# Weight chunks streamed as three tiles, the last weight split in place and later, and two kinds of fetch issued behind the chunks, in a two-layer graph network kernel

## Chip, core and metric

The kernel runs on one core of one Trainium2 chip. The metric is device time in microseconds for one execution of the whole program, here given as the median of three runs. The profile is that of one further execution, with the hardware profiler on.

## What is computed

The input is `x` with 32 graphs of 512 nodes and 512 features, and one adjacency `adj` of 512 x 512 that holds zeros and ones. Layer 0 is masked attention with 8 heads of 64 lanes, layer 1 a graph convolution; both add their input and normalise. Cut to what matters:

```python
q, k, v = (x @ W + b for W, b in ((Wq, bq), (Wk, bk), (Wv, bv)))       # 8 heads of 64
scores = q @ k.T / sqrt(64) + where(adj == 0, -1e9, 0)
x = layernorm(x + softmax(scores) @ v)
y = adj @ x
x = layernorm(x + y @ weight + bias)
```

## The kernel before

**Three passes.** A float32 product is made of three passes of TensorE matmuls at a reduced format. Each operand is split into three parts, named HIGH, REST and BOTH, and the passes multiply like parts: HIGH and REST add into a bank called near, BOTH into a bank called far. A split takes a scaled copy on ScalarE (HIGH), a combination on VectorE or GpSimd (REST), and one more, for the activations on GpSimd (BOTH). `one_pass` (line 417) issues four matmuls of 128 x 128 by 128 x 512, `three_passes` twelve.

**Chunks.** Wq and Wk are split once, at the start, into eight chunks in the order q0, k0, q1, k1, q2, k2, q3, k3 (`SEQUENCE`). A chunk is 768 KB: its three parts, of 256 KB each, in one tile of 6 KB per partition. `keep_chunk` (L404) stores each to DRAM as one transfer, and in every later graph `fetch_chunk` (L412) brings it back, as one transfer, into a ring of three tiles named `stream` (`AHEAD = 3`). The fetch of the chunk three places on is written directly after the matmuls that used the ring's oldest tile, so it waits for all twelve of them. The last three chunks of a graph are followed by the fetches of q0, k0, q1 for the next graph, which stand near the end of an iteration.

**Order of work.** The order on every engine is written out by hand (`manual_schedule`), and each engine runs its list in order. `iteration(b)` mixes the end of graph b's attention, the projections and first scores of graph b+1, and the convolution of graph b-1. TensorE's order in it is: attention with values for head pairs 0 and 1 (`attend`, L625); scores of the second group of head pairs (`scores`, L602); projections q0 to k1 of graph b+1 (L417); attention for head pairs 2 and 3; scores of graph b+1's first group; projections q2 to k3; values (L417 from `wv`); aggregation with the adjacency (L526); convolution with the last weight (L417 from `w`).

**Scores.** A score stage has 16 products into a ring of eight banks. VectorE empties each bank with the mask into an `e` tile (L604), ScalarE takes the exponential of each pair of them (L606), GpSimd adds the exponentials over the key blocks (L617). VectorE folds those sums in squares of 32 x 32 (`fold_squares`, L655 and L657); they go to DRAM and back to come to the right partitions (`pass_parts` L664, `fetch_parts` L671), and `add_up` (L677, L678) makes the inverse.

**Rows.** The attention's output comes out transposed. `turn_out` transposes it in squares on VectorE (L637) and stores it to DRAM (L639), `fetch_rows` (L645) reads it back as four transfers of 64 KB for each head pair, ScalarE scales it (L691) and GpSimd adds it to x (L695).

**SyncE's queue.** Nearly all transfers are issued by SyncE, in the order of the code, and one that waits holds up all behind it. In iteration b the order is: the two `turned` stores, `fetch_parts`, eight rows transfers, in iterations 2 to 5 an adjacency row (`load_adjacency_rows`, L290, looked at by L296 to L298 for a low half), the chunks k1, q2, k2, a store of the output, q3, then `load(b)`, k3, the squares of x for graph b+2 (16 transfers, L232), eight more rows transfers, and q0, k0, q1 for the next graph.

**The start.** Graph 0's projections use the chunks as they are made. Then come graph 0's first scores, its values, and the splits of x for graph 1 (L304 HIGH on ScalarE, L307 REST on VectorE, L310 BOTH on GpSimd), the first `fold_squares`, and the split of the last weight `W1` into `w1`: `load_last_weight` (L750) loads it as four tiles of 256 KB into room of the q and k tiles, `split_last_weight` does for each of four row blocks three ScalarE activations (L757, L758, L760, the last into a spare tile) and two GpSimd subtractions (L761, L762). All this stands ahead of iteration 0. `AFTER[b]` holds units that the next iteration runs between the transposes of its first two head pairs.

Of the kernel before, what the change touches and what calls it, by code (L numbers as in the profile page):

```python
# [8 lines left out]
FP = mybir.dt.float32  # L9
# [9 lines left out]
P = 128  # L19
# [163 lines left out]
def fast_kernel(ctx: ExitStack, tc, verdict, x, adj, Wq, bq, Wk, bk, Wv, bv, W1, b1, out):  # L183
# [20 lines left out]
    def plain(t):  # L204

        return t.bitcast(FP)
# [164 lines left out]
    MADE = {}  # L371

    def chunk():
        return work.tile([P, 3, DB, P], FR, name="stream", bufs=AHEAD)

    def make_chunk(n):

        which, m = SEQUENCE[n]
        if n < DB:
            made = early[:, n, :, :, :]  # L380
        elif n < DB + AHEAD:
            made = chunk()
        else:
            made = last_chunk
        MADE[n] = CHUNK[0, which, m] = made
        high_of_weight(made[:, HIGH, :, :], RAW[which, m // 2][:, m % 2, :, :])

    def rest_of_chunk(n):
        which, m = SEQUENCE[n]
        made = MADE[n]  # L390
        rest_of_weight(made[:, REST, :, :], made[:, HIGH, :, :], RAW[which, m // 2][:, m % 2, :, :])

    def both_of_chunk(n):
        made = MADE[n]
        both_of_weight(made[:, BOTH, :, :], made[:, HIGH, :, :], made[:, REST, :, :])

    def finish_chunk(n):
        rest_of_chunk(n)
# [1 line left out]

    def keep_chunk(n):
        which, m = SEQUENCE[n]
        KEPT[which, m] = passing.tile([P, 3, DB, P], FP, name=f"kept_{which}{m}", bufs=1)
        nc.sync.dma_start(KEPT[which, m], plain(MADE.pop(n)))  # L404

    def fetch_chunk(n):

        b, (which, m) = n // len(SEQUENCE), SEQUENCE[n % len(SEQUENCE)]
        if b >= B:
            return  # L410
        CHUNK[b, which, m] = chunk()
        nc.sync.dma_start(plain(CHUNK[b, which, m]), KEPT[which, m])  # L412

    def one_pass(f, pm, left, right, blocks=range(DB)):

        for d in blocks:
            nc.tensor.matmul(pm, left(f, d), right(f, d), start=(f != REST and d == 0),  # L417
                             stop=(f != HIGH and d == DB - 1))
# [12 lines left out]
    def project(b, which, m):  # L431

        n = b * len(SEQUENCE) + SEQUENCE.index((which, m))
        near, far = bank(N), bank(N)
        w, xt = CHUNK.pop((b, which, m)), XT[b]
        three_passes(near, far, lambda f, d: w[:, f, d, :], lambda f, d: xt[f][:, d, :])
        if b == 0:
            return [(finish_projection, b, which, m, near, far)]
        if (which, m) in SEQUENCE[:-AHEAD]:
            fetch_chunk(n + AHEAD)  # L440
        finish_projection(b, which, m, near, far)

    def project_first_two():

        ends = []
        xt = XT[0]
        for which, m in SEQUENCE[:2]:
            ends.append((CHUNK[0, which, m], bank(N), bank(N)))
        for f in (HIGH, REST, BOTH):
            for w, near, far in ends:  # L450
                one_pass(f, far if f == BOTH else near, lambda f, d: w[:, f, d, :], lambda f, d: xt[f][:, d, :])
# [189 lines left out]
    def fetch_rows(b, hp):  # L641
        rows = ROWS[b, hp] = work.tile([P, NB, P], FP, name="rows")
        turned = TURNED.pop((b, hp)).rearrange("(i r) (c j f) -> j r c i f", r=SQ, c=NB, f=SQ)
        for j in range(P // SQ):
            nc.sync.dma_start(rows[j * SQ:(j + 1) * SQ, :, :].rearrange("p c (i f) -> p c i f", f=SQ), turned[j])  # L645
# [99 lines left out]
    both_of_chunk(1)  # L745

    def load_last_weight():
        for d in range(DB):
            RAW["w1", d] = work.tile([P, D], FP, name="raw", tag="qk"[d % 2] + "0", bufs=PAIRS)
            nc.sync.dma_start(RAW["w1", d], W1[d * P:(d + 1) * P, :])  # L750

    def values_weight(d):
        return RAW["v", d // 2][:, d % 2, :]

    def split_last_weight(d):
        w = RAW.pop(("w1", d))
        nc.scalar.activation(w, w, AF.Copy, scale=1.0 / EPSILON)  # L757
        nc.scalar.activation(w1[:, HIGH, d, :], w, AF.Copy, scale=SHRINK)  # L758
        temp = work.tile([P, N], FR, name="temp", tag="turn", bufs=TURNS)
        nc.scalar.activation(temp, w, AF.Copy, scale=EPSILON * SHRINK)  # L760
        nc.gpsimd.tensor_sub(w1[:, REST, d, :], w, plain(w1[:, HIGH, d, :]))  # L761
        nc.gpsimd.tensor_sub(w1[:, BOTH, d, :], plain(w1[:, REST, d, :]), plain(temp))  # L762

    def norm(t, which):

# [30 lines left out]
    def iteration(b):  # L796
# [16 lines left out]
            fetch_parts(b, 0)  # L813
        take_scores(b, 1)
        run(later)
        fetch_rows(b, 0)
        fetch_rows(b, 1)
        look = []
        if 2 <= b < 2 + NB:
            load_adjacency_rows(b - 2)  # L820
            look = [(look_for_low_half, b - 2)]
        if b == 0:
            run(merge(units[:4], [[(fold_squares, b, 1), (pass_parts, b, 0), (fetch_parts, b, 0)], [], [(add_up, b, 0)],
                                  folded[:1]]))
        else:
            old, young = norm(b - 1, 1), norm(b - 1, 0)
            roots = slice(0, 2 * NB if b > 1 else NB)
            if b == 1:
                run(survey(0, 0))
            run(merge(units[:4], [[(square_root, b - 1, roots), (add_up, b, 0), (invert_root, b - 1, roots)],  # L830
                                  folded[:1] + old[2:], [(store, b - 2)] if b > 1 else [], young[2:] + scaled]))
        attend(b, 2)
        turn_out(b, 2)
        load(b)
        attend(b, 3)
        turn_out(b, 3)
        if b == 0:
# [9 lines left out]
                          turned[:1] + (later_added if b == B - 2 else [])]))  # L847
        if b == B - 2:
            load(B - 1)
        run(merge(gathered, [[unit] for unit in turned[1:]]))  # L850
        fresh, seen, shift = survey(b, 0), survey(b - 1), biases(b - 1)
        high, rest, both = divided
# [166 lines left out]
```

## Time and profile before

| What | Value |
|---|---|
| Median of three runs | 2574.64 us (2574.56 to 2575.02) |
| The profiled execution | 2578.16 us |
| Span of the profiled execution, first to last instruction | 2575.9 us |
| Mean granted TensorE clock | 0.999 |
| SyncE's transfers, share of 16 DMA engines | 51.3%, 377.48 MB |
| Chunk fetches (L412) | 248 of 768 KB, 3.9 / 4.7 / 10.1 us to landing (least, median, most) |
| Rows transfers (L645) | 496 of 64 KB, median 2.4 us to landing |
| Loads of the last weight (L750) | 4 of 256 KB, median 8.6 us to landing |

A line of the page's fifth part or of a timeline reads: line of the code, engine, operation, what is written and what is read by the program's names, shapes, and how often. A timeline line begins with the start and the length in us, neighbours of one kind merged; in brackets is the engine's idle time before it and what ended it. PE is TensorE, DVE is VectorE, ACT is ScalarE, POOL is GpSimd, SPq is SyncE's queue, whose length is that of the issue alone. One score product counts as two matmuls in the trace.

### The profile page before, as it was taken

What the parts mean: (1) busy time and instruction counts of PE and PEld (TensorE: products, weight loads), DVE (VectorE), ACT (ScalarE), POOL (GpSimd) and SP (SyncE); (2) the same over time, 40 slices, a digit from 0 to 9 for tenths busy, and PEclk for the clock granted to TensorE, in tenths of its full rate; (3) what the DMA queues carried; (4) which work ended last, traced back from release to release, by engine and by line L of the source; (5) the groups of instructions that cost most, each with busy time, mean ns of one, the idle gap of its engine ahead of it and who ended that gap; (6) DMA issues with size and microseconds to landing.
All of it is one profiled execution on the core that took longest, in us unless ns stands there. A gap on an engine that the chain in (4) does not pass through costs nothing.

```text
span 2575.9 us, 35702 instructions
## 1 busy us (share of the span) xinstructions
PE 2562.7 (99%) x11324; PEld 1693.9 (66%) x11324; DVE 2058.9 (80%) x3795; ACT 1527.3 (59%) x2540; POOL 1751.0 (68%) x1105
## 2 busy tenths in 40 slices
PE   9999999999999999999999999999999999999998
PEld 6566666766667666666667666676766667666666
DVE  8778788787787887878878778887788787887878
ACT  5666655657556665556665566655656556565555
POOL 5766676666766666766667667676766766666767
PEclk9999999999999999999999999999999999999999
DMA  9655554655545545456454464454654545545431
GB/s 267 165 158 142 159 146 125 174 140 162 148 112 167 152 151 162 110 154 176 135 160 119 143 178 136 153 138 129 172 141 161 143 117 167 145 157 164 103 124 52
DMA packets 675042, 380.47 MB, mean 148 GB/s; under 512 B 586912, under 2 KB 591264, under 8 KB 674848
## 3 DMA queue, kind: packets, MB, share of 16 engines
q1 hardware_dynamic: 674416, 377.48, 51.3%
q8 instruction: 92, 1.51, 0.2%
q14 instruction: 102, 0.84, 0.1%
q10 hardware_dynamic: 432, 0.66, 0.1%
HBM read 303.57 MB, written 74.45 MB: 147 GB/s over the span
## 4 chain that ended last, share of the span: by engine, by line
PE 94%; DVE 2%; DMA 1%; POOL 1%; ACT 1%; issue 0%; SPq 0%; DVEq 0%; ACTq 0%; POOLq 0%
PE bank L417 52%; PE bank L602 17%; PE bank L625 16%; PE bank L526 9%; DVE e L604 1%; DMA stream<-kept_k 0%; DMA turned<-attT 0%; DVE bnst L477 0%; DVE factors L307 0%; POOL es L617 0%; ACT e L606 0%; SPq L645 0%; POOL factors L310 0%; PE bank L729 0%; POOL wv L932 0%
## 5 line engine op out<-in xcount | busy, mean ns | idle before, releaser
L417 PE MATMUL bank<-factors,stream 128*128 128x512 f32 x3012 | 704.3, 392 | 2.9 <-DMA stream<-kept_k 2.3
L606 ACT ACTIVATE e<-e 128x1024 f32<-128x1024 f32 x512 | 525.3, 1055 | 300.7 <-DVE e L604 262.3
L417 PEld LDWEIGHTS bank<-factors,stream 128*128 128x128 f32 x3012 | 560.1, 188 | 167.7 <-DVE e L604 23.5
L617 POOL TENSOR_TENSOR es<-es,e 128x1024 f32<-128x1024 f32 x256 | 615.9, 2406 | 20.1
L604 DVE SCALAR_TENSOR_TENSOR e<-gap,bank 128x512 f32<-128x512 uint8 x1024 | 617.6, 678 | 12.1 <-PE bank L602 12.1
L617 POOL TENSOR_TENSOR es<-e 128x1024 f32<-128x1024 f32 x128 | 305.8, 2389 | 425.6 <-ACT e L606 425.6
L602 PE MATMUL bank<-q,k 64*128 64x512 f32 x2048 | 464.9, 598 | 0.7 <-DVE attT L637 0.7
L625 PE MATMUL bank<-e,v 128*64 128x512 f32 x2048 | 453.6, 595 | 0.0
L602 PEld LDWEIGHTS bank<-q,k 64*128 64x128 f32 x2048 | 204.1, 186 | 259.9 <-issue 157.3
L417 PE MATMUL bank<-w,factors 128*128 128x512 f32 x1536 | 354.4, 389 | 0.5 <-POOL factors L310 0.5
L417 PE MATMUL bank<-wv,factors 128*128 128x512 f32 x1536 | 353.5, 389 | 0.0
L310 POOL TENSOR_TENSOR factors<-factors,factors 128x512 fp32r<-128x512 f32 x255 | 322.1, 1284 | 33.9 <-DVE factors L307 32.0
L691 ACT ACTIVATE rows<-rows,zero,inverse 128x64 f32<-128x64 f32 x992 | 335.0, 429 | 9.7 <-DVE inverse L678 9.7
L417 PEld LDWEIGHTS bank<-w,factors 128*128 128x128 f32 x1536 | 288.0, 188 | 61.3 <-POOL factors L310 1.3
L417 PEld LDWEIGHTS bank<-wv,factors 128*128 128x128 f32 x1536 | 288.2, 188 | 60.6 <-DVE e L604 0.8
L625 PEld LDWEIGHTS bank<-e,v 128*64 128x64 f32 x2048 | 141.4, 137 | 278.4 <-issue 265.4
L503 ACT ACTIVATE high<-xs 128x512 fp32r<-128x512 f32 x124 | 74.4, 627 | 333.3 <-PE bank L526 333.2
L504 POOL TENSOR_TENSOR low<-xs,high 128x512 fp32r<-128x512 f32 x124 | 159.2, 1295 | 156.3 <-PE bank L526 156.3
L541 POOL TENSOR_TENSOR xs<-xs,b_r 128x512 f32<-128x512 f32 x124 | 159.8, 1289 | 125.3 <-DVE xs L561 125.3
L637 DVE STREAM_TRANSPOSE attT<-bank 128x512 f32<-128x512 f32 x124 | 87.6, 708 | 159.1 <-PE bank L625 159.1
L493 ACT ACTIVATE xs<-xs,shift,rstd 128x512 f32<-128x512 f32 x248 | 181.5, 805 | 14.7 <-DVE shift L488 14.7
L695 POOL TENSOR_TENSOR xs<-xs,rows 128x512 f32<-128x512 f32 x124 | 160.6, 1306 | 22.6 <-ACT rows L691 14.9
(98 smaller groups left out, 2433.4 us busy)
## 6 DMA issues: line engine op xcount, KB each, us to landing
stream<-kept_q SPq DMA_DIRECT2D x124, 768.0 KB, 5.9
stream<-kept_k SPq DMA_DIRECT2D x124, 768.0 KB, 4.3
xin<-in_x_dram SPq DMA_DIRECT2D x496, 64.0 KB, 2.3
turned<-attT SPq DMA_DIRECT2D x124, 256.0 KB, 3.2
rows<-turned SPq DMA_DIRECT2D x496, 64.0 KB, 2.4
xs<-in_x_dram SPq DMA_DIRECT2D x31, 1024.0 KB, 6.1
out_dram<-xs SPq DMA_DIRECT2D x31, 1024.0 KB, 5.1
part<-passed SPq DMA_DIRECT2D x256, 8.0 KB, 1.7
```

Of the source, the lines that this page charges most:

```text
L310: engine.tensor_sub(both, plain(high), plain(rest))
L417: nc.tensor.matmul(pm, left(f, d), right(f, d), start=(f != REST and d == 0), stop=(f != HIGH and d == DB - 1))
L493: nc.scalar.activation(row, row, AF.Identity, bias=SHIFT[t][:, slot:slot + 1], scale=RSTD[t][:, slot:slot + 1])
L526: nc.tensor.matmul(pm, part, adjT[:, n % NB, :], start=(n == 0), stop=(n == 2 * NB - 1))
L541: nc.gpsimd.tensor_add(X[b][:, c, :], X[b][:, c, :], b1_r)
L602: nc.tensor.matmul(ps[s], keys[:, j * P:(j + 1) * P], queries, start=True, stop=True)
L604: nc.vector.scalar_tensor_tensor(e[:, s, :], gap[:, j, :], NEG * root, ps[s], op0=ALU.mult, op1=ALU.add)
L606: nc.scalar.activation(e, e, AF.Exp, scale=1.0 / root)
L617: nc.gpsimd.tensor_add(ES[b, hp], ES[b, hp] if j > 1 else E[b, hp, 0], E[b, hp, j])
L625: nc.tensor.matmul(po[s * HD:(s + 1) * HD, :], V[b, j][:, h * HD:(h + 1) * HD], e[:, s, :], start=(j == 0), stop=(j == NB - 1))
L691: nc.scalar.activation(part, part, AF.Identity, bias=zero, scale=inverse[:, c, s:s + 1])
L695: nc.gpsimd.tensor_add(cols, cols, ROWS.pop((b, hp)))
```

## The change

Four edits. A chunk becomes three tiles, each with a ring of three (`stream0`, `stream1`, `stream2`) and a transfer of its own, to DRAM and back. The last weight is loaded as one tile of 1 MB into the ring of the x tiles (`xs`), its split runs in iteration 0 behind graph 1's values, and BOTH is made from HIGH, scaled back into the raw tile in place, where a third copy of the raw weight was used. Ahead of iteration 0 only HIGH of graph 1's x is split; REST and BOTH run in iteration 0 between the first two transposes. And in iteration 1 both rows fetches, in iterations 2 to 5 the second of them, are issued behind the first projection with its chunk fetch, and the adjacency row behind `load(b)`.

```diff
     def chunk():
-        return work.tile([P, 3, DB, P], FR, name="stream", bufs=AHEAD)
+        return [work.tile([P, DB, P], FR, name=f"stream{f}", bufs=AHEAD) for f in (HIGH, REST, BOTH)]
...
     def keep_chunk(n):
         which, m = SEQUENCE[n]
-        KEPT[which, m] = passing.tile([P, 3, DB, P], FP, name=f"kept_{which}{m}", bufs=1)
-        nc.sync.dma_start(KEPT[which, m], plain(MADE.pop(n)))
+        KEPT[which, m] = [passing.tile([P, DB, P], FP, name=f"kept_{which}{m}_{f}", bufs=1) for f in range(3)]
+        for kept, made in zip(KEPT[which, m], MADE.pop(n)):
+            nc.sync.dma_start(kept, plain(made))
...
         CHUNK[b, which, m] = chunk()
-        nc.sync.dma_start(plain(CHUNK[b, which, m]), KEPT[which, m])
+        for part, kept in zip(CHUNK[b, which, m], KEPT[which, m]):
+            nc.sync.dma_start(plain(part), kept)
...
-        three_passes(near, far, lambda f, d: w[:, f, d, :], lambda f, d: xt[f][:, d, :])
+        three_passes(near, far, lambda f, d: w[f][:, d, :], lambda f, d: xt[f][:, d, :])
...
     def load_last_weight():
-        for d in range(DB):
-            RAW["w1", d] = work.tile([P, D], FP, name="raw", tag="qk"[d % 2] + "0", bufs=PAIRS)
-            nc.sync.dma_start(RAW["w1", d], W1[d * P:(d + 1) * P, :])
+        RAW["w1"] = work.tile([P, DB, D], FP, name="xs", bufs=2)
+        nc.sync.dma_start(RAW["w1"], W1.rearrange("(c p) f -> p c f", p=P))
...
-    def split_last_weight(d):
-        w = RAW.pop(("w1", d))
-        nc.scalar.activation(w, w, AF.Copy, scale=1.0 / EPSILON)
-        nc.scalar.activation(w1[:, HIGH, d, :], w, AF.Copy, scale=SHRINK)
-        temp = work.tile([P, N], FR, name="temp", tag="turn", bufs=TURNS)
-        nc.scalar.activation(temp, w, AF.Copy, scale=EPSILON * SHRINK)
-        nc.gpsimd.tensor_sub(w1[:, REST, d, :], w, plain(w1[:, HIGH, d, :]))
-        nc.gpsimd.tensor_sub(w1[:, BOTH, d, :], plain(w1[:, REST, d, :]), plain(temp))
+    def split_last_weight():
+        w = RAW["w1"]
+        for d in range(DB):
+            nc.scalar.activation(w[:, d, :], w[:, d, :], AF.Copy, scale=1.0 / EPSILON)
+            nc.scalar.activation(w1[:, HIGH, d, :], w[:, d, :], AF.Copy, scale=SHRINK)
+            nc.gpsimd.tensor_sub(w1[:, REST, d, :], w[:, d, :], plain(w1[:, HIGH, d, :]))
+        for d in range(DB):
+            nc.scalar.activation(w[:, d, :], plain(w1[:, HIGH, d, :]), AF.Copy, scale=EPSILON)
+            nc.gpsimd.tensor_sub(w1[:, BOTH, d, :], plain(w1[:, REST, d, :]), w[:, d, :])
...
         take_scores(b, 1)
         run(later)
-        fetch_rows(b, 0)
-        fetch_rows(b, 1)
-        look = []
-        if 2 <= b < 2 + NB:
-            load_adjacency_rows(b - 2)
-            look = [(look_for_low_half, b - 2)]
+        waiting = [(fetch_rows, b, 0), (fetch_rows, b, 1)]
+        looking = 2 <= b < 2 + NB
+        look = [(look_for_low_half, b - 2)] if looking else []
+        ready = 1 if looking else 0 if b == 1 else 2
+        run(waiting[:ready])
...
-            run(merge(units[:4], [[(square_root, b - 1, roots), (add_up, b, 0), (invert_root, b - 1, roots)],
+            run(merge(units[:4], [waiting[ready:]
+                                  + [(square_root, b - 1, roots), (add_up, b, 0), (invert_root, b - 1, roots)],
...
         load(b)
+        if looking:
+            load_adjacency_rows(b - 2)
         attend(b, 3)
...
         if b == B - 2:
             load(B - 1)
+        if b == 0:
+            split_last_weight()
         run(merge(gathered, [[unit] for unit in turned[1:]]))
...
     high, rest, both = splits_of_x(1)
-    run(high + rest + both[::-1])
-
+    run(high)
     fold_squares(0, 0)
-    run([(split_last_weight, d) for d in range(DB)])
+    AFTER[-1] = (rest + both[::-1], [])
     for b in range(B - 1):
         iteration(b)
```

More of the change, by code (lines that the diff above doesn't have):

```diff
@@ L379, in make_chunk @@
         if n < DB:
-            made = early[:, n, :, :, :]
+            made = [early[:, n, f, :, :] for f in (HIGH, REST, BOTH)]
         elif n < DB + AHEAD:
@@ L383, in make_chunk @@
         else:
-            made = last_chunk
+            made = [last_chunk[:, f, :, :] for f in (HIGH, REST, BOTH)]
         MADE[n] = CHUNK[0, which, m] = made
-        high_of_weight(made[:, HIGH, :, :], RAW[which, m // 2][:, m % 2, :, :])
+        high_of_weight(made[HIGH], RAW[which, m // 2][:, m % 2, :, :])
     def rest_of_chunk(n):
@@ L390, in rest_of_chunk @@
         made = MADE[n]
-        rest_of_weight(made[:, REST, :, :], made[:, HIGH, :, :], RAW[which, m // 2][:, m % 2, :, :])
+        rest_of_weight(made[REST], made[HIGH], RAW[which, m // 2][:, m % 2, :, :])
     def both_of_chunk(n):
         made = MADE[n]
-        both_of_weight(made[:, BOTH, :, :], made[:, HIGH, :, :], made[:, REST, :, :])
+        both_of_weight(made[BOTH], made[HIGH], made[REST])
     def finish_chunk(n):
@@ L450, in project_first_two @@
             for w, near, far in ends:
-                one_pass(f, far if f == BOTH else near, lambda f, d: w[:, f, d, :], lambda f, d: xt[f][:, d, :])
+                one_pass(f, far if f == BOTH else near, lambda f, d: w[f][:, d, :], lambda f, d: xt[f][:, d, :])
         return [(finish_projection, 0, which, m, near, far) for (which, m), (w, near, far) in zip(SEQUENCE, ends)]
```

## The prediction, made before the changed kernel was run

> **What bounds the kernel now.** I read the page first: busy shares and the chain of work that ended last.
>
> ```profile
> span 2575.9 us, 35702 instructions
> PE 2562.7 (99%) x11324; PEld 1693.9 (66%) x11324; DVE 2058.9 (80%) x3795; ACT 1527.3 (59%) x2540; POOL 1751.0 (68%) x1105
> ...
> PE 94%; DVE 2%; DMA 1%; POOL 1%; ACT 1%; issue 0%; SPq 0%; DVEq 0%; ACTq 0%; POOLq 0%
> ```
>
> TensorE is the bound. A change that leaves its matmuls alone can only win the time in which it stands still or is held back, and busy time hides some of that, so I read the TensorE timeline next, taking a stage's length as the distance between two starts.
>
> ```profile
> 56.91 8.27 PE L602 MATMUL bank<-q,k 64*128 64x512 f32 x32
> 65.11 11.17 PE L417 MATMUL bank<-factors,stream 128*128 128x512 f32 x48
> ...
> 83.23 2.85 PE L602 MATMUL bank<-q,k 64*128 64x512 f32 x12
> 86.74 6.48 PE L602 MATMUL bank<-q,k 64*128 64x512 f32 x20 [0.66 <-DVE attT L637]
> 93.15 11.22 PE L417 MATMUL bank<-factors,stream 128*128 128x512 f32 x48
> ...
> 122.19 7.21 PE L602 MATMUL bank<-q,k 64*128 64x512 f32 x32
> 129.33 8.49 PE L417 MATMUL bank<-factors,stream 128*128 128x512 f32 x36
> 139.52 2.97 PE L417 MATMUL bank<-factors,stream 128*128 128x512 f32 x12 [1.70 <-DMA stream<-kept_k]
> 142.42 7.09 PE L625 MATMUL bank<-e,v 128*64 128x512 f32 x32
> ```
>
> From iteration 6 on every stage repeats (scores 7.14, first four projections 11.15, period 79.6), so nothing is to be had there. The excess lies in the first iterations: scores from 56.91 take 8.20 (**A**, 1.06 over), scores from 83.23 take 9.92 (**B**, 2.78 over), projections from 129.33 take 13.09 (**C**, iteration 1, 1.94 over). Read the same way, the stages at 210.89, 290.77 and 450.84 (iterations 2, 3, 5) take 11.42, 12.03 and 11.93: 0.27, 0.88 and 0.78 over (**D**, 1.93). Sum 7.71 us, or 0.30%.
>
> Who is late in A and B is in the VectorE and then the ScalarE timeline:
>
> ```profile
> 51.24 4.41 DVE L307 SCALAR_TENSOR_TENSOR factors<-factors,turn 128x512 fp32r<-128x512 f32 x4
> ...
> 59.18 9.61 DVE L604 SCALAR_TENSOR_TENSOR e<-gap,bank 128x512 f32<-128x512 uint8 x16
> ...
> 82.60 0.27 DVE L677 TENSOR_REDUCE inverse<-part 128x16 f32<-128x64 f32 x1 [3.38 <-DMA part<-passed]
> ...
> 87.20 9.62 DVE L604 SCALAR_TENSOR_TENSOR e<-gap,bank 128x512 f32<-128x512 uint8 x16
> ```
>
> ScalarE:
>
> ```profile
> 59.85 0.63 ACT L757 ACTIVATE raw<-raw 128x512 f32<-128x512 f32 x1 [7.88 <-DMA raw<-in_L_gnn_weight_dram]
> ...
> 66.68 7.68 ACT L606 ACTIVATE e<-e 128x1024 f32<-128x1024 f32 x8
> ```
>
> A score stage has 16 products and eight banks, and L604 empties one per 0.60. In undisturbed stages the first L604 starts 1.16 after the stage (122.19 to 123.35, 203.75 to 204.91). In A it is 2.27, in B 3.97: 1.11 and 2.81 more, the same as the excess within 0.05. So **a score stage loses what its first L604 is late beyond 1.16**. In B the root is the split of the last weight: ScalarE waited 7.88 for it and worked at it until 66.68, exponentials and q, k came after it, VectorE's q at 74.96, the sums' round trip through DRAM (part<-passed) at 82.60.
>
> C is in SyncE's timeline:
>
> ```profile
> 121.40 1.97 SPq L639 DMA_DIRECT2D turned<-attT  x2
> ...
> 129.07 5.32 SPq L645 DMA_DIRECT2D rows<-turned  x8
> 134.48 0.57 SPq L412 DMA_DIRECT2D stream<-kept_k  x1
> ```
>
> The eight rows transfers stand ahead of the fourth chunk (k1). It is issued 5.15 after the stage starts, lands after 4.90 at 139.38, and TensorE resumes 0.14 later. In iterations 2, 3 and 5 the chunk is issued on time (at 213.94, 293.86, 453.93) but takes 5.3 to 5.9 behind rows and the adjacency row; it too lands 0.14 before its use. Iteration 4 takes 4.59 and iteration 7 3.97, and there nothing waits.
>
> **What the Trainium skill says.** "TensorE: Matmul & The Clock Gate", "Back-to-back issue gap", gives N/2.4 + 2.5 ns for one warm matmul, 216 ns at 512 columns; the trace has 48 in 10.88 us, 227 ns each, so undisturbed stages have little left. "SBUF — State Buffer", "SBUF: two separate sides": VectorE with two SBUF inputs and GpSimd exclude each other for a whole instruction. The trace agrees: the first L307 at 51.24 lasts 2.60, until GpSimd's L617 is over, the next ones 0.67. "DMA: Bandwidth & Descriptors", "Anatomy of one DMA": about 2 us fixed per transfer, mostly the write's receipt (stated for another issuing path). Here 8 KB takes 1.7, 64 KB 2.3 to 2.4, 256 KB 3.1 to 3.2, 768 KB 4.3 to 5.9: the same shape, so a third of a chunk lands over a microsecond sooner than a whole one.
>
> **The change, part by part.** *Start, A.* VectorE now does the square fold first, then a transpose of the first head pair, then the four L307, then the second transpose. From the turn's end at 51.31: fold 1.29 + 1.23, to 53.8; transpose 0.7, to 54.5 (its product ends at 53.4); four L307 at 0.61, to 57.0, for GpSimd is done at 53.3 and its next instruction waits for them; second transpose after its product, 57.1 to 57.8. First L604 at 56.91 + 1.16 = 58.07: the excess of 1.06 goes. The cover is 0.3 us. What may eat it: the eight stores become 24 transfers ahead of the squares of x, and the last square landed at 50.52, just before its turn at 50.61. In the built program each SyncE transfer also waits for the landing of the eighth before it. I bound the delay by 0 and 1.5 us, so A gives 0 to 1.06; I take 0.9.
>
> *B.* The split leaves ScalarE, so its exponentials follow L604 (to 67.7) and end at 68.9; q on VectorE at 69.6 instead of 74.96; fold (2.5) to 72.7; part's way took 82.60 - 78.02 = 4.6, so sums at 77.3, k to 78.5, fold to 81.0, transposes 81.7 and 83.0. The stage starts at 82.1, L604 can start at 83.26: the excess of 2.78 goes with 0.6 to spare. GpSimd has 10.3 us less ahead of it (8 x 1.29), so its four L310, now from 57.0, end at 62.0, 4 before the third pass wants them. Between 1.0 and 2.78; I take 2.7.
>
> *The split where it is now*, after the values of iteration 0: 12 ScalarE activations (7.4 us; 4 x 3 as before) and 8 GpSimd subtractions (10.3). With everything 3.84 earlier, ScalarE's last q,k ends at 100.4, GpSimd's sums of exponentials at 104.1. GpSimd does four subtractions to 109.6 and four to 114.8; ScalarE waits for the first four one by one in its second loop and ends at 110.2. Queued behind it are the splits of x(2) at 112.8, rows and exponentials: 2.6 to spare. GpSimd's 114.8 meets VectorE's L307 at 114.4: a port wait of 0.4, where VectorE stood idle 0.94 before its second transpose. Cost 0, and 1:1 if GpSimd is over 0.5 later; upper bound 1. The weight is used at 186. Its transfer, one instead of four, waits for the last chunk's store (landed 46.5, issue at 51.3): nothing.
>
> *C and D.* In iteration 1 both rows fetches, in 2 to 5 the second, go behind the first projection; 8 or 4 issues of 0.65 each leave the stretch ahead of k1. The adjacency row goes behind the load of x, 1 issue of 0.62, at about 228.6 to 229.2, and the next in that queue, a transpose's store, comes at 230.19; it lands near 236 and is read at 242. The rows then issue from 2.8 to 8.1 after the stage's start and land by 10; ScalarE reads them at 15.7 (145.03). The chunks queued behind them are wanted 25 after it. k1's first tile is free after one pass, 1.0 after the stage's start, and wanted at 8.16: 7 us for 256 KB. All of 1.94 + 1.93; I take 3.8.
>
> *Three tiles in all iterations.* 16 more transfers per iteration, 5.3 to 6.1 us of SyncE at 0.33 to 0.38. The first two of a chunk issue while SyncE used to wait for the third pass; nine in a row at an iteration's end take 2.5 more where SyncE then waits for 15 (182.87 to 201.18). Three packets of 2 KB take 3 x 93 ns, one of 6 KB 272: 2.6% more of the chunks' DMA time, unseen. TensorE gets 16 more waits per iteration: 0, as the chunk starts inside a stage are already waits and keep 227 ns, to 114 ns, the bubble after a stage's first matmul (341 against 227). I take 0. k3, which has 0.8 to 1.3 to spare each time, gains over 2.
>
> Sum: 0.9 + 2.7 + 3.8 = 7.4, or **2570.8** against the profiled 2578.16 (span 2575.9 and 2.3 around it). The median, 2574.64, is 3.5 below the profiled run, so some waits may be shorter there; I take nine tenths, 6.8, an estimate: **2567.8**.
>
> **The rivals.** (1) As worked out, 2565.8 to 2569.4: chance 0.70. (2) Part only: the 3.5 us lie in C and D, which then are small in ordinary runs, or B keeps a microsecond from a late part transfer. For it: landings of 0.14 before use show how finely C and D hang on DMA. Against: A and B are program order. 7.4 - 3.5 = 3.9, 2570.7: 0.18. (3) It does not do what it says: the squares land late, A and B stay, C and D are small; within 2 us, near 2573.5: 0.07. (4) Slower: the added waits at each pass break TensorE's overlap with its weight loads. 31 x 16 = 496 waits; at the full 114 ns 56.5 us, 2624. It decides from 6.8/496 = 14 ns each. Against it: the third passes wait for VectorE's bank today without a gap. 0.05.
>
> **How the numbers follow.** About 0.2% (5.1 us, 2569.5) can be told from no change. Faster is case 1, 0.70; same cases 2 and 3, 0.25; slower 0.05. The range starts at 2565.8 (all 7.7, the first score stage's 0.5, 0.6 for the landings) and ends at 2571.6, which takes in most of case 2.
>
> **What would show it.** Scores of A and B at 7.14 with L604 1.16 behind; the split between 100 and 115 and the score stage behind it at 7.14; iterations 1 to 5 at 11.15; period 79.6 after that. I am wrong if the first L604 of A or B stays late, if a gap stands at second or third passes, or if the period grows.

## The result, and the profile after

| | Before | After |
|---|---|---|
| Median, run in turn on one chip | 2574.43 us (2573.55 to 2575.56, 16 runs) | 2569.51 us (2568.52 to 2570.28, 16 runs) |
| Profiled execution | 2578.16 us | 2569.8 us |
| Its span | 2575.9 us | 2568.0 us |

The ratio is 0.9981, with a 95% interval of 0.9974 to 0.9988: the change saves 4.9 us (3.1 to 6.7), about 0.19%. The two profiles show 7.9 between them. The 3.0 that they show too much is a part of the story below. Of the executions of the kernels below, three took far longer than the others of their kernel (3242 and 2877 us of after_all at a granted clock of 0.75 and 0.85, 5301 us of tiles_order at 1.0), and the medians and ratios given are those without them.

Lines of the changed kernel behind L404, which is now L405, lie two further down than before: L412 is L414, L417 is L419, L602 is L604, L604 is L606, L637 is L639, L639 is L641, L645 is L647.

The page of the kernel after, its span and shares and the chain of work that ended last:

```profile
span 2568.0 us, 36900 instructions
...
PE 2558.3 (100%) x11324; PEld 1693.7 (66%) x11324; DVE 2057.4 (80%) x3795; ACT 1528.6 (60%) x2540; POOL 1751.0 (68%) x1105
...
PE 97%; SPq 1%; DVE 1%; DMA 1%; issue 0%; POOL 0%; ACT 0%; DVEq 0%
```

TensorE's share of the chain rises from 94% to 97%, as it should when its waits go. Where they went is in its timeline after (start, length, idle time before in brackets):

```profile
57.00 8.63 PE L604 MATMUL bank<-q,k 64*128 64x512 f32 x32
65.57 8.46 PE L419 MATMUL bank<-factors,stream 128*128 128x512 f32 x36
74.27 2.98 PE L419 MATMUL bank<-factors,stream 128*128 128x512 f32 x12 [0.24 <-DMA stream<-kept_k]
...
84.20 7.21 PE L604 MATMUL bank<-q,k 64*128 64x512 f32 x32
...
120.34 7.21 PE L604 MATMUL bank<-q,k 64*128 64x512 f32 x32
127.48 11.20 PE L419 MATMUL bank<-factors,stream 128*128 128x512 f32 x48
138.61 7.09 PE L627 MATMUL bank<-e,v 128*64 128x512 f32 x32
```

Read by the distance of two starts: C, now at 127.48, takes 11.13 without a stall. B, now at 84.20, takes 7.14 and has lost nothing; so does the score stage behind the split's new place, at 120.34. But A, at 57.00, takes 8.56, which is more than before, and the projections behind it have a stall that was not there. In a table, with what each stage takes over its undisturbed length (7.14 for scores, 11.15 for these projections), and with one more execution of each kernel from the experiments:

| Lost in | Before | Before, again | After | After, again |
|---|---|---|---|---|
| A, scores near 57 | 1.06 | 1.04 | 1.42 | 1.22 |
| projections near 65 (11.10 undisturbed) | 0 | 0 | 0.51 | 0.46 |
| B, scores near 83 | 2.78 | 2.50 | 0 | 0 |
| C, iteration 1 | 1.94 | 1.01 | 0 | 0 |
| D, iterations 2 to 5 | 1.93 | 0.24 | 0 | 0 |
| small losses: the other projections of chunks, each over 11.10 or 11.01 by at most 0.13, added up | 2.19 | 2.22 | 0.15 | 0.72 |

The first five rows give 5.8 of the 7.9 between the first and the third column, the last row 2.0. The loss added in the first two rows, and the last row, were not foreseen.

**Why B and C are gone.** VectorE's first L606 of B, and SyncE's queue in iteration 1:

```profile
85.36 9.66 DVE L606 SCALAR_TENSOR_TENSOR e<-gap,bank 128x512 f32<-128x512 uint8 x16 [0.33 <-PE bank L604]
```

```profile
128.71 2.16 SPq L414 DMA_DIRECT2D stream<-kept_k  x3
130.96 6.11 SPq L647 DMA_DIRECT2D rows<-turned  x8
```

In B the first L606 is 1.16 behind the stage's start, and the wait before it is for TensorE's bank. In C the three parts of k1 are issued ahead of the rows, the first of them 1.23 after the stage's start, and the last has landed at 133.43; TensorE begins on them at 135.80.

**Why A is late.** VectorE after, from the last turn of a square of x to the first L606:

```profile
53.01 0.71 DVE L347 STREAM_TRANSPOSE turn<-xin 128x512 f32<-128x512 f32 x1 [1.48 <-DMA xin<-in_x_dram]
...
56.62 2.45 DVE L307 SCALAR_TENSOR_TENSOR factors<-factors,turn 128x512 fp32r<-128x512 f32 x4
58.99 0.71 DVE L639 STREAM_TRANSPOSE attT<-bank 128x512 f32<-128x512 f32 x1
59.63 3.04 DVE L606 SCALAR_TENSOR_TENSOR e<-gap,bank 128x512 f32<-128x512 uint8 x5
```

From the turn on everything runs in the new order without idling (four L307 in 2.45, not the 4.41 of before), but the turn itself waited 1.48 for its squares, which landed at 52.99 where they had landed at 50.52. The first L606 comes 2.63 after the stage's start, 1.47 beyond 1.16, and the stage loses 1.42.

**Why the projections near 65 are late.** SyncE's queue after (length is the issue alone):

```profile
44.33 5.67 SPq L232 DMA_DIRECT2D xin<-in_x_dram  x8
...
54.98 0.46 SPq L751 DMA_DIRECT2D xs<-in_L_gnn_weight_dram  x1
56.73 3.33 SPq L641 DMA_DIRECT2D turned<-attT  x2
64.78 5.84 SPq L647 DMA_DIRECT2D rows<-turned  x8
70.72 1.52 SPq L414 DMA_DIRECT2D stream<-kept_k  x3
```

The megabyte of the last weight is issued at 54.98 and lands at 64.08. The `turned` store issued at 56.73 lands at 64.77, the rows that read it back wait for it on SyncE until 64.78, k1's tiles stand behind them, and the first lands at 74.13. In a stage without a stall TensorE begins on the fourth chunk 8.29 after the stage's start, which would be 73.86 here; it begins at 74.27, 0.14 after the landing.

### The profile page after: what moved, and what is told of

It reads as the page before. It is cut to its first block, busy times and chain, and to the rows that moved or that the text cites. A ratio compares the mean times of both kernels' runs of the same rounds, so it can differ in the third digit from the quotient of the medians.

```text
span 2568.0 us, 36900 instructions
## 1 busy us (share of the span) xinstructions
PE 2558.3 (100%) x11324; PEld 1693.7 (66%) x11324; DVE 2057.4 (80%) x3795; ACT 1528.6 (60%) x2540; POOL 1751.0 (68%) x1105
## 3 DMA queue, kind: packets, MB, share of 16 engines
q1 hardware_dynamic: 748096, 377.51, 53.6%
q8 instruction: 93, 1.52, 0.3%
## 4 chain that ended last, share of the span: by engine, by line
PE 97%; SPq 1%; DVE 1%; DMA 1%; issue 0%; POOL 0%; ACT 0%; DVEq 0%
PE bank L419 54%; PE bank L604 17%; PE bank L627 17%; PE bank L528 9%; SPq L405 0%; DMA turned<-attT 0%; SPq L232 0%; SPq L647 0%; DVE bnst L479 0%; POOL factors L310 0%; PE bank L731 0%; DMA xin<-in_x_dram 0%; DMA stream<-kept_k 0%; PE bank L336 0%; DVE xlast L563 0%
## 5 line engine op out<-in xcount | busy, mean ns | idle before, releaser
L419 PE MATMUL bank<-factors,stream 128*128 128x512 f32 x3012 | 701.3, 392 | 0.2 <-DMA stream<-kept_k 0.2
L419 PEld LDWEIGHTS bank<-factors,stream 128*128 128x128 f32 x3012 | 560.5, 188 | 161.7 <-DVE e L606 23.5
L606 DVE SCALAR_TENSOR_TENSOR e<-gap,bank 128x512 f32<-128x512 uint8 x1024 | 617.9, 681 | 12.5 <-PE bank L604 12.5
L604 PE MATMUL bank<-q,k 64*128 64x512 f32 x2048 | 463.3, 598 | 0.0
L604 PEld LDWEIGHTS bank<-q,k 64*128 64x128 f32 x2048 | 203.5, 186 | 258.3 <-issue 172.2
L419 PE MATMUL bank<-w,factors 128*128 128x512 f32 x1536 | 354.4, 389 | 0.5 <-POOL factors L310 0.5
L419 PE MATMUL bank<-wv,factors 128*128 128x512 f32 x1536 | 353.5, 389 | 0.0
L419 PEld LDWEIGHTS bank<-w,factors 128*128 128x128 f32 x1536 | 288.0, 188 | 61.3 <-POOL factors L310 1.3
L419 PEld LDWEIGHTS bank<-wv,factors 128*128 128x128 f32 x1536 | 288.2, 188 | 60.6 <-DVE e L606 0.8
L639 DVE STREAM_TRANSPOSE attT<-bank 128x512 f32<-128x512 f32 x124 | 87.9, 709 | 155.0 <-PE bank L627 152.1
```

Of the source, the lines that this page charges most:

```text
L604: nc.tensor.matmul(ps[s], keys[:, j * P:(j + 1) * P], queries, start=True, stop=True)
L606: nc.vector.scalar_tensor_tensor(e[:, s, :], gap[:, j, :], NEG * root, ps[s], op0=ALU.mult, op1=ALU.add)
```

## The experiments

Three groups of four kernels, each group on a chip of its own with the kernel before in turn with them; ratios are to that. The theory: B, C and D go by the edits that the prediction named; A stays late because 24 stores now stand ahead of the squares of x; the new stall is the megabyte ahead of the `turned` stores. The rivals: A is late by VectorE's own new order; the stall comes from the fold's transfers moved in front of it; and what the two profiles differ by is in part no work of the change.

### First group: the parts alone

**before_again**, no edit.

> The kernel before, unchanged, for a second profile. The profiled execution of before (2578.2 us, span 2575.9) was 3.7 us above the median of its 16 runs (2574.4). Theory: what varies from run to run are the waits for chunk k1 in iterations 1, 2, 3 and 5 (C and D of the prediction, 3.87 us in that execution), which hang on DMA; then an ordinary execution has a span near 2572.5, A and B as before (8.2 and 9.9 us stages) and C and D together under 1 us. Rival: C and D are there in every execution (3 to 4 us in sum) and the slow execution lost its time elsewhere; then a span near 2572.5 shows another stage shorter.

2575.81 us in this execution, span 2573.6, A 1.04, B 2.50, C 1.01, D 0.24. A and B are the program's. C and D are the execution's: 1.3 here, 3.9 in the profile that I predicted from, although k1 is issued late in both (at 133.94 here, landing at 138.49, TensorE resuming at 138.62). The trace puts this last wait down to VectorE's L429 on k, which ends at 138.57. But in iterations without a stall that instruction ends 8.89 after the stage's start and TensorE has begun on the fourth chunk at 8.33, so it is the chunk that is waited for.

**tiles_only**, the chunk functions of the diff and nothing else:

```diff
-        KEPT[which, m] = passing.tile([P, 3, DB, P], FP, name=f"kept_{which}{m}", bufs=1)
-        nc.sync.dma_start(KEPT[which, m], plain(MADE.pop(n)))
+        for kept, made in zip(KEPT[which, m], MADE.pop(n)):
+            nc.sync.dma_start(kept, plain(made))
```

> The kernel before with only the three tiles, rings and transfers per chunk. Theory: D goes and most of C, for the first third of k1 lands earlier; B stays at 2.8 us over; the start loses, since 24 stores push the last squares of x from 50.5 to about 53, so that the first L604 of stage A comes about 2 us later than before (stage A 9 to 10 us). The 0.04 us that each projection stage of the changed kernel is shorter (1.7 us over the program) shows here. Net between -1 and +1 us against before. Rival: the three tiles cost per iteration (period over 79.6 us) or the 0.04 us belongs to another edit; then stages of 11.15 and 11.05 stay.

2577.41 against 2576.52, ratio 1.0002 (0.9994 to 1.001). A 1.05, B 4.23, the projections near 65 0.34 (a wait for ScalarE's q at their end, not for a chunk), C 1.49, D none. So thirds of a chunk alone bring nothing: they remove D, and pay for it in B, whose split waits for a weight that is now issued behind 24 stores (first part issued at 55.06 and landed at 61.69, 51.28 and 59.83 before). C's stall now stands ahead of the third pass, whose part, behind the eight rows, lands at 142.78, 0.13 before TensorE resumes. A is no longer than before, against what I expected, though the last square landed at 52.02.

**split_only**, the new split and the new order of VectorE at the start (cut to the order):

```diff
-    run(high + rest + both[::-1])
-
+    run(high)
     fold_squares(0, 0)
-    run([(split_last_weight, d) for d in range(DB)])
+    AFTER[-1] = (rest + both[::-1], [])
```

> The kernel before with only the last weight loaded as one tile and split behind the values, and REST and BOTH of x(1) moved into iteration 0. Chunks are one tile and one transfer as before. Theory: the squares land at 50.5 as before, so A goes too (8.20 to 7.2) as the prediction worked out, B goes (9.92 to 7.14), C and D stay as in an ordinary execution: 3.8 us faster. Rival: A's lateness in the changed kernel comes from the new order on VectorE itself, not from the stores; then A stays at 8.2 to 8.6 and the gain is 2.5 us.

2573.19, ratio 0.9986 (0.998 to 0.9993). A 0, B 0.28, C 1.28, iterations 2 to 5 together 0.8. TensorE in it:

```profile
57.69 7.21 PE L602 MATMUL bank<-q,k 64*128 64x512 f32 x32
64.83 11.21 PE L417 MATMUL bank<-factors,stream 128*128 128x512 f32 x48
75.98 7.09 PE L625 MATMUL bank<-e,v 128*64 128x512 f32 x32
82.99 7.49 PE L602 MATMUL bank<-q,k 64*128 64x512 f32 x32
```

This is the part that saves most. And it answers the first rival: with VectorE's new order, and the eight stores of before, A is gone. That A goes by the order and B by the place of the split is read from the timelines; the two were not run apart. The megabyte stands ahead of the `turned` stores here too, and the projections at 64.83 lose nothing: it is issued at 50.85, behind three fetches of whole chunks and not nine of thirds, and lands at 61.24. So the new stall takes the megabyte and the later issue together.

**order_only**, rows and adjacency behind the chunks:

```diff
-        fetch_rows(b, 0)
-        fetch_rows(b, 1)
+        run(waiting[:ready])
...
+        if looking:
+            load_adjacency_rows(b - 2)
```

> The kernel before with only the rows and adjacency fetches issued later. Theory: C and D go, A and B stay: what they are worth in ordinary runs is this kernel's gain, about 0.5 to 1.5 us if the median differs from the profiled execution by them, 3.9 us if they are there in every run (rival).

2575.34, ratio 0.9997 (0.9989 to 1.0005). C gone, B 1.66, but iterations 2 to 5 still lose 0.06, 0.57, 0.25 and 0.38, and iteration 9 0.48. B is smaller because the last weight's first part landed at 58.78 here; over the kernels with the old split B follows that landing (1.47 behind A's start here; 2.92 for B's 2.78 before, 4.47 for 4.23 in tiles_only).

### Second group: what is late in A and behind it

**after_stores**, the change with chunks whose parts lie side by side stored in one transfer, so that 14 stores stand ahead of the squares:

```diff
+        if whole_chunk is not None:
+            nc.sync.dma_start(kept, plain(whole_chunk))
+        else:
+            for part, made in zip(KEPT[which, m], parts):
+                nc.sync.dma_start(part, plain(made))
```

> The change, but the eight made chunks go to DRAM in one transfer where their tiles lie side by side (q0, k0, q1, k1, k3), so that 14 stores stand ahead of the squares of x instead of 24. My theory for A (scores at 57.0 take 8.56, 1.42 over): the 24 stores take SyncE 0.65 each and the squares land at 53.0 instead of 50.5. Then the squares land about 51 here, L308 of the third factors no longer ends late, and the scores near 57 take 7.2 to 7.5, with k1 of iteration 0 still about 0.5 late behind the last weight's load; about 1 us less than the change, ratio to before near 0.9977. Rival: A is late by VectorE's own new order (fold and transposes), not by the squares; then A stays at 1.0 to 1.4 over and the stores only move idle time.

2568.46, ratio 0.9978 (0.997 to 0.9986). The last square landed at 50.26 and A is 0, as the theory says. The projections near 65 lose 0.80, more than the 0.5 expected: the megabyte, still ahead of the `turned` stores, lands at 63.36 and k1's first tile at 73.14.

**after_late_load**, the change with the load of the last weight moved:

```diff
-    load_last_weight()
...
         turn_out(b, 2)
+        if b == 0:
+            load_last_weight()
         load(b)
```

> The change, but the last weight (1 MB) is fetched in iteration 0 behind the third head pair's transposes instead of ahead of the values. My theory for the new 0.51 in the projections at 65.6: turned<-attT lands at 65 behind that megabyte, rows and k1 after it. Then turned lands near 61 to 62, k1 lands before its use, and those projections take 11.1; A stays 1.4 over; about 0.5 less than the change. Rival: k1 is late because the second square fold and its stores now issue later on SyncE; then 0.3 to 0.5 over remains. Loaded there the weight must still come before its split at about 100, or the scores at 120 grow.

2568.23, ratio 0.9977 (0.9967 to 0.9986). The projections near 65 take 11.10. SyncE's queue in it:

```profile
54.29 3.75 SPq L641 DMA_DIRECT2D turned<-attT  x2
60.36 5.43 SPq L647 DMA_DIRECT2D rows<-turned  x8
65.89 1.52 SPq L414 DMA_DIRECT2D stream<-kept_k  x3
```

Without the megabyte between, the rows start at 60.36 where they started at 64.78, and k1 is issued 4.8 earlier. Some of that is A, which is not late here; after_stores, where A isn't late either and the megabyte stands ahead, issues its rows at 64.01. The scores at 118.26 take 7.14: the weight comes in time for its split. But A is 0 too, with all 24 stores, against what I expected: here the squares landed at 50.41. The fetch that was moved is issued after them, so it can't be the reason.

**after_all**, both edits, and `ready` 0 in iteration 0 as well.

> Both edits (14 stores, late fetch of the last weight), and both rows fetches of iteration 0 behind its first projection as the change has it in iteration 1. If the causes of A and of the new k1 stall are as I say, and add up: scores near 57 at 7.2 to 7.5, projections near 65 at 11.1, 1.7 to 1.9 us less than the change, ratio to before near 0.9974. Rival: one wait takes the place of another (a transfer or VectorE in the values or scores that follow), and less than half of that is gained.

2568.83, ratio 0.9976 (0.9967 to 0.9984). Neither A nor the projections near 65 lose anything, 0.18 comes back in the scores at 82.42. Over the stages of the table's first five rows that is 1.75 less than after. The medians don't show that the two edits add up: on this chip after_stores has 2568.46 and after_late_load 2568.23.

**tiles_order**, three tiles and the order of rows, without the split.

> Three tiles and the new order of rows and adjacency, without the new split. Two questions. First C and D: gone, as with the order alone, and now also in iterations 3, 5 and 9 where the order alone left 0.3 to 0.6, because a third of a chunk lands sooner: 11.1 each. A stays about 1.05 over and B 2 to 4 over. Second, the 0.04 to 0.05 us by which each later projection stage is shorter with the change and with none of its parts alone (sum over the program about 2.1): if tiles and order together make it, it is here (rest of the stream stages 0.1 to 0.3 over in sum); if it needs the split, or is a thing of one execution, it is not (2.2 over, as in each part). Ratio to before 0.9985 to 1.0.

2573.73, ratio 0.9996 (0.9987 to 1.0005). The stages of C and D take 11.10 in all five iterations. A 1.06, B 4.02. The sum of small losses in the projections of chunks is 0.21, which I took for a sign that tiles and order together shorten later stages. The third group shows that it isn't.

### Third group: repeats, and the squares first

**after_again**, the change unaltered.

> The changed kernel once more, unaltered, on the same chip as its neighbours. Question: is A's 1.42 over (squares landed at 52.99) what 24 stores always cost, or one execution? With 24 stores the last square landed at 50.41, 51.24, 52.02 and 52.99 in four executions, with 14 at 49.83 and 50.26, with 8 at 50.48, 50.52 and 51.33. Up to about 51.2 of it is covered. If the stores only thin the margin, A is anywhere from 0 to 1.4 here, with L604's counterpart late as the square is; if they set it, A is 1 to 1.4 again. The projections at 65 stay 0.3 to 0.8 over in either case, since the order of the queue makes that. C, D at 11.1, later stages 11.10 and 11.01.

2569.60, ratio 0.9979 (0.9971 to 0.9988). Last square at 52.51, A 1.22, projections near 65 0.46.

**late_load_again**, as after_late_load.

> The change with the last weight fetched in iteration 0, once more, beside the change on one chip. The cause of the stall at 65 is settled if those projections take 11.1 again. A should depend on the landing of the squares as in the change, since this fetch is issued after them: 0 to 1.4 over. Ratio to before 0.0002 to 0.0005 under that of the change run beside it; rival: equal, if ordinary runs of the change don't have the stall.

2569.17, ratio 0.9977 (0.997 to 0.9985). The projections near 65 take 11.12, so that cause is settled twice, the second time with A late. A loses 0.43, with the last square at 52.49.

**squares_late**, the late fetch of the weight, and the last two squares issued ahead of the stores of five chunks (15 of the 24 stores; the expectation counts them wrongly as three chunks and 9):

```diff
+    for d in range(2, DB):
+        load_squares(1, d)
     for n in range(AHEAD, len(SEQUENCE)):
         keep_chunk(n)
-    for d in range(2, DB):
-        load_squares(1, d)
```

> Late fetch of the last weight, and the last two squares of x issued ahead of the last three chunks' stores (9 of the 24 stores behind them). If the place of the squares in the queue is A's cause, they land near 45 to 48, VectorE's fourth turn waits for no transfer, and the scores near 57 take 7.14 in this and any execution. Rival: A is VectorE's own order, then 7.5 or more. The chunks fetched behind the stores land 1 to 2 later than now (51.4 to 59.0), and are wanted from 64. Total as the late fetch alone at its best, ratio near 0.9976; it would be the fastest, by a few tenths of a microsecond at most.

2568.66 (2568.16 to 2569.03), ratio 0.9975 (0.9965 to 0.9984); on the same chip the change has 2569.60 (2568.73 to 2570.56). Spans 2566.4 and 2568.0. The squares land by 40.92, earlier than I expected, and VectorE no longer waits for one:

```profile
50.46 0.70 DVE L347 STREAM_TRANSPOSE turn<-xin 128x512 f32<-128x512 f32 x1
...
54.08 2.45 DVE L307 SCALAR_TENSOR_TENSOR factors<-factors,turn 128x512 fp32r<-128x512 f32 x4
56.88 0.72 DVE L639 STREAM_TRANSPOSE attT<-bank 128x512 f32<-128x512 f32 x1 [0.34 <-PE bank L627]
57.92 2.48 DVE L606 SCALAR_TENSOR_TENSOR e<-gap,bank 128x512 f32<-128x512 uint8 x4 [0.33 <-PE bank L604]
```

The turn has no bracket now, and the brackets behind it name TensorE: VectorE waits for the bound engine, not the other way. The first L606 is 1.16 behind the stage's start at 56.76, and the stage takes 7.14. Its advantage over the change is 0.9 in the medians and 1.6 in the traces (1.22 in A and 0.46 behind it); the intervals of the two ratios overlap. Nor can it be told from after_stores, after_late_load and after_all, whose ratios are 0.9976 to 0.9978.

**tiles_only_again**, as tiles_only.

> Three tiles alone, a second execution, for the later projection stages: 11.15 and 11.05 in this kernel, in the order alone, the split alone and twice in before; 11.10 and 11.01 in the change, its three variants, and in tiles with order, although TensorE's instructions there are the same one by one from iteration 6 on. If it belongs to the kernel, 11.15 and 11.05 again (2.2 over in sum); if it belongs to an execution, 11.10 and 11.01 may come up here. A 1.05, B 3 to 4, C 1 to 1.5 over.

2576.16 in this one execution; A 1.85, B 4.18, C 0.99, D none. A is longer than the 1.05 expected: the last square landed at 53.56, behind an issue that took SyncE 1.37 (from 48.04), so 24 stores can make A late in VectorE's old order too. The small losses are 0.65, where the same kernel had 2.23 on the first chip.

### What the three groups say together

*A is a question of when the last square lands.* Over all kernels with VectorE's new order:

| Kernel | Stores ahead of the last square | Landed | Scores start | A over |
|---|---|---|---|---|
| the change | 24 | 52.99 | 57.00 | 1.42 |
| after_again | 24 | 52.51 | 56.73 | 1.22 |
| late_load_again | 24 | 52.49 | 57.50 | 0.43 |
| after_late_load | 24 | 50.41 | 56.86 | 0 |
| split_only | 8 | 51.33 | 57.69 | 0 |
| after_stores | 14 | 50.26 | 57.16 | 0 |
| after_all | 14 | 49.83 | 57.16 | 0 |
| squares_late | 9 | 40.92 | 56.76 | 0 |

In the three that lose, the landing lies 4.01, 4.22 and 5.01 ahead of the scores, and landing and loss add up to 5.43, 5.44 and 5.44: A loses what the square is late beyond 5.44 ahead of its stage, 1:1, as it must when VectorE doesn't idle between the turn and the first L606. All that lose nothing landed 6.36 or more ahead.

*Why 24 stores make it late in some executions only.* In the change, 15 stores ahead of the last eight squares take SyncE from 34.57 to 44.22, 0.64 each; five took it from 34.77 to 39.27 before. So the last eight squares were issued from 39.38 to 47.41 before and are issued from 44.33 to 49.52 now, the last of them 2.1 later. Before, the first five of them took SyncE 1.1 to 1.8 each, and that cost nothing, as the stores ahead of them were landing until 46.48. Now each is issued only 2.5 to 3.5 ahead of its landing, with few transfers in flight, and when one issue takes longer (46.93 to 48.41), the DMA engines run out of work. The DMA view of the change from 46 to 52 us, 40 slices of 0.15, busy tenths and GB/s:

```profile
DMA  9988999557339941000026974686589888949448
GB/s 198 193 152 137 167 187 214 89 86 111 53 54 181 178 56 11 9 10 12 3 42 104 170 110 78 101 134 93 88 136 169 140 129 141 168 66 160 50 147 314
```

From 48.25 to 49.15 the engines stand nearly empty. The repeat of the change has such a hole at the same place behind an issue from 47.35 to 48.43; after_late_load has no issue over 0.9 among its squares, and no hole. But the hole is not the whole cause. Before has one as well, from 48.7 to 49.6, behind the issue of the last square itself (47.41 to 48.88), and that square was in time. And late_load_again has no hole: there an issue near the start took 2.22 (from 9.22; 0.82 in after_late_load), and the squares were issued from 45.91, 2.0 later than in after_late_load, when the scores were only 0.64 later. So what the 24 stores take away is the margin, and which delay then reaches A differs from execution to execution. What makes SyncE take over 1 us for a single issue isn't shown by any run.

*The small losses go with the chip, not with the kernel.* They add up to 2.20 to 2.34 in all four kernels of the first group, 0.15 to 0.22 in the second, 0.64 to 0.72 in the third, and tiles_only, the change and the late fetch each moved with the chip. The clock is not it: the values take 10.88 and undisturbed scores 7.14 in the profiles of every group. Each chip was used at one time only, so chip and moment can't be told apart. The profile of before has 2.19, that of after 0.15. So 2.0 of the 7.9 us between those two profiles is no effect of the change; medians taken in turn on one chip don't have it.

## Why the prediction was right, and where it was not

The direction, and a time inside the range, came out of the steps for B, C and D. Its central value is 1.7 too low: 6.8 us forecast, 4.9 measured (the rest is the median of before, 2574.43 and not 2574.64). The measured 2569.51 lies just outside the first case, which ends at 2569.4; the range holds it because it also takes in most of the second. So that the number fits is in part luck. The first case came true for B, a part of the third for A (the squares land late), and C and D went, but a second profile of before has them small, as the second case says.

- **The rule** (a score stage loses what its first L604 is late beyond 1.16) held in every score stage of the profiles that lost anything, within 0.05: 2.63 behind the start for a loss of 1.42 after, 1.16 for none in B, in the stage at 120.34 and in squares_late.
- **Start, A**: the failed step. "I bound the delay by 0 and 1.5 us, so A gives 0 to 1.06; I take 0.9." The delay was 2.5 in the profile after and 2.0 in its repeat, A gave nothing and lost another 0.16 to 0.36. VectorE's new order works as laid out (split_only: A 0). What failed is the price of 16 more transfers on SyncE: the step named them, and named the cover of 0.3, but bounded the squares' delay without counting 15 issues of 0.64 where there were five that took 4.5 together. The cover came out larger, 0.95: squares may be late to 5.44 ahead of the stage, and the 50.52 of before is 6.39 ahead of 56.91. The delay was larger still.
- **B**: 2.7 taken, 2.78 and 2.50 lost before, 0 after. First L606 at 85.36, 1.16 behind the start at 84.20. With the split alone 0.28 stayed in its one profile. With B gone the third rival, that nothing changes, is out.
- **The split where it is now**: cost 0 forecast, and 0 measured. ScalarE works at it from 102.23 to 112.45, GpSimd from 106.71 to 116.73, 1.9 later than worked out, as B too starts 2.1 later than worked out, and the stage behind takes 7.14. The port wait of 0.4 came out as 0.17 (the first L307 there, at 116.44, takes 0.85, the next three 0.68).
- **A step that was missing**: the last weight's transfer. The working says "nothing" for it; it asked what the transfer waits for, and not what waits behind it. One megabyte instead of four quarters, now issued 1.7 ahead of the first `turned` store and behind nine fetches, cost 0.46 to 0.51 in both executions.
- **C and D**: the mechanism was right, 0 is left of them. That it takes two edits was not seen: order alone leaves up to 0.57 in iterations 3 to 5, tiles alone leave 1.0 to 1.5 in C, and only both together are clean. The size was off as the second rival said: 3.9 in the profile of before, 1.3 in its repeat, 2.0 in split_only, which kept them whole.
- **Three tiles in all iterations**: 0 forecast. No gap stands at second or third passes, and no stage from B on is over 0.04 longer than before, so the fourth rival is out. The transfers of SyncE's queue take 53.6% of the DMA engines' time and not 51.3%, 2.3 points more, where the working's 2.6% of the chunks' time comes to 0.6 points; TensorE doesn't feel it. The gain in k1's landing rested on the Trainium skill's page "DMA: Bandwidth & Descriptors", section "Anatomy of one DMA", according to which a transfer has a fixed part of about 2 us and a part that grows with its bytes (stated there for transfers that GpSimd issues). The traces agree: in iterations 2, 3 and 5 of tiles_only, with the rows ahead as before, k1's first third landed 3.2 to 3.9 after its issue, where whole chunks had taken 5.3 to 5.9 in D; with the new order as well, in iteration 2 after, the thirds took 2.6 to 2.8.
- **Nine tenths**: the profile of before was 3.5 over its median, and the deduction was meant for that. Two causes can now be named, C and D (3.9 against 1.3) and the chip (2.0 in the small losses), but how an ordinary run of before divides between them was not measured. An estimate from the repeat, which lost 1.25 in C and D and ran 0.7 under its chip's median of 2576.52: about 2 for C and D, if all that varies is theirs.

The sum: A came out 1.0 to 1.2 below what was left of it after the nine tenths (0.8 taken, 0.16 to 0.36 lost), the stall of the weight 0.5. That is 1.5 to 1.7 of the 1.9 missing. With C and D at the estimated 2, where nine tenths of 3.8 were taken, 1.4 more would be missing than that; the interval of 3.1 to 6.7 for the gain is too wide to say more.

## What to carry to other kernels

When a transfer is cut in three, count the issues on the queue, and look at who is served behind them: issue time first uses up the margin between a landing and its reader, and once the margin is gone each further delay reaches the reader. Of a large load ask what is queued behind it, not only what it waits for itself. And read one profiled execution as a sample: of the stalls before, those of program order (A, B) came back within 0.3, those that hang on a landing by 0.1 us (C, D) came back at a third; and after the change A hangs on a landing too.

## What was not expected of the hardware

- The same kernel takes 11.15 and 11.05 for its projections of chunks on one chip, 11.10 and 11.01 on another, with the same granted clock of 0.999; over the program that is 2 us, two fifths of what this change is worth.
- Stores of 256 KB issued back to back took SyncE 0.64 each here, fetches of 256 KB 0.44 to 0.5 (three in 1.33 to 1.52), so the sum of issues is not the same for both directions in this stretch.
- Single issues among the squares took 1.1 to 1.8 us where their neighbours took 0.5. Before, with the large stores still in flight, five of them cost nothing; after, one was enough to empty the DMA engines for 0.9 and put the squares behind it 1 us later.
